# A two-layer transformer kernel: another order of the beginning, and the common row added beside the routed tiles

## The chip, the cores and the metric

The kernel runs on one core of a Trainium2 chip. The time is device microseconds (us) of one execution of the whole program, the median of several runs. TensorE (PE in the profile) does the matrix products; DVE, ACT and POOL are the vector, scalar and GpSimd engines; SP only issues transfers. ACT and POOL issue transfers of their own as well, each on a queue of its own.

## The reference

The activations x are 2 x 2048 rows (tokens) of 256 numbers. Two layers are applied, and each adds an attention part and a feed-forward part, both computed from the same normed input:

```python
xn = layernorm(x)
x = x + L0_attention(xn) + L0_ffn(xn)       # causal, one head, biases bq, bk, bv
xn = layernorm(x)
x = x + L1_attention(xn) + L1_ffn(xn)       # causal, then a block on selected tokens

def L0_ffn(xn):                             # mixture of experts
    scores = softmax(xn @ gate_w + gate_b)  # 8 experts, the best 2 of each token
    routed = sum(weight * expert(xn))       # silu(xn@w1+b1) * (xn@w2+b2) @ w3 + b3
    shared = mean over 2 shared experts     # same form, sw1, sb1, ... sb3
    return shared + routed
```

All of it is in float32. Layer 1's attention is causal over stretches of 512 tokens, and its feed-forward part works on the selected tokens alone. Neither is touched by the change.

## The kernel before

The tokens are held on the chip in eight blocks of 512 (`x_blocks`, four rows of 128 per block); blocks 0 to 3 are the first sequence, 4 to 7 the second. A tile is 128 tokens.

**The start (0 to 33 us).** `load_x` (L75) loads all eight blocks by SP. Two square weights, wq and wk, come by ACT's queue (L178), are transposed on TensorE (L409) and copied by ACT (L410). Scores need only their product wa (L491), so that keys are the normed input itself. The biases bq and bk lead to the small products of L433 and L438 and from these to a column `ca`, a scalar `qk_bias` and one more column of the value weights (L442 to L444, DVE). The value weights `wvg` hold wv, the gate's weights and this column. `every` is a row that is added to all tokens: the mean of the two shared experts' output biases, and bv (L421 to L424, POOL).

`moments` computes mean and variance of blocks (L205, L206, DVE), then the inverse root by a chain of small DVE operations (`rsqrt`, L189 to L194) and a shift (L214). `layernorm` makes the normed rows xn with ACT (L227), and turns them on TensorE (L233) into xnT. `prepare0(g)` calls it for block g, copies the normed rows as 16-bit halves for the scatter (L506, POOL), adds `every` to the block (L508, POOL, one operation of 128x1024), and makes values, gate scores and the score shift in four products, one for each j (L515), followed by `shift` (L523) and `logits` (L524) for the whole block. `evacuate` copies a result out of PSUM with DVE (L154) and ACT (L156) in turn. `project_q0` makes the queries of a block (L650, L654).

**Layer 0's attention (33 to 349 us).** It goes tile by tile: 0 to 15 of the first sequence, then 15 to 0 of the second. Scores come from L257, the row maximum from L268 and L274 (DVE), exp from L276 (ACT). The exponentials of the first four tiles are turned on TensorE (L321); for all others POOL splits them into two planes (L310), SP's queue transposes these by DMA (L312) into `across`, and DVE and ACT join them to pT (L287, L288). L332 multiplies with the values, L344 adds to x.

What else must be done in this time is a generator, `side0`: moments and `prepare0` of the other blocks (1 to 3 in one group, 4 to 7 in the next), the routing (`route_experts`), 64 scatters of rows on POOL (L636), and the fetch of the first two expert tiles. `beside()` takes steps of it at set rates (`BESIDE_L0`: 2.0, 1.2 and 0.72 steps per piece of attention); a step that yields `HOLD` keeps the instructions of the next step behind attention's latest ones. `before_tile` takes further steps until the values for a tile are there, and lets ACT's queue issue transfers from `clear()` that fill scratch memory with zeros (L454 and after; 13 of 768 KB, then others, then bias rows of the experts): two for each tile up to (0,7), then one.

**Routed experts (349 to 700 us).** 36 planned tiles of up to 256 rows. POOL joins the fetched rows to xT (L714), TensorE makes the two products of L722, ACT and DVE their activation and product (L836, L837), and TensorE the output (L844, DVE L849). The first tile's L722 products are interleaved with the end of attention (`fill_with_first`).

**After it** come the shared experts (to 1120 us) with layer 1's routing beside them, and layer 1 (to the end).

Between engines the order follows from data; within one engine it follows from the order in which the code is written and from manual dependencies.

## Time and profile before

| | us |
|---|---|
| median of 3 runs | 1507.68 (1506.83 to 1508.04) |
| the profiled execution's own time | 1504.37 |
| its span in the profile | 1502.7 |
| TensorE busy | 1453.6 |
| DVE busy | 696.2 |
| ACT busy | 437.5 |
| POOL busy | 401.2 |
| first values (L515) | 23.45 |
| first scores (L257) | 33.28 |
| first routed tile wholly after attention (L722) | 351.23 |

The profile holds one execution. Start times in it count from the start of its span. A matrix product in float32 leaves two records, a transpose one. TensorE's clock can be throttled; the granted clock is shown as a share of full speed (1.00), and its mean over the execution was 0.997. The time that an engine stands idle before an instruction is put down to whatever released it last.

### The profile page before, as it was taken

The numbers are of one execution on the slowest core, as the hardware profiler recorded it, in microseconds if no ns is written. First come the engines' busy times: TensorE is split into PE (matmuls) and PEld (weight loads), VectorE is DVE, ScalarE is ACT, GpSimd is POOL, SyncE is SP. The second block draws the span as 40 slices with busy tenths as digits, with TensorE's granted clock in tenths as the row PEclk, the third lists the DMA queues.
The fourth block names the chain that finished last, engine by engine and source line by source line (L and its number), as shares of the span: only waits on it lengthen the run. The fifth ranks groups of instructions, "written<-read, shape, count | busy, mean of one in ns | idle before, by whom it ended". The sixth has DMA issues, their size and how long they took to land.

```text
span 1502.7 us, 17818 instructions
## 1 busy us (share of the span) xinstructions
PE 1453.6 (97%) x5816; PEld 1033.6 (69%) x5816; DVE 696.2 (46%) x2064; ACT 437.5 (29%) x827; POOL 401.2 (27%) x581
## 2 busy tenths in 40 slices
PE   7989999999999999999999999999999998999999
PEld 4666666668888888887565656566675765667656
DVE  6437333443222222222424447766546458666354
ACT  2443333332111111111121121115524533344233
POOL 3454777531111111111201221132013122421122
PEclk9999999999999999999999999999999999999999
DMA  4744665586887989873101111130005435621153
GB/s 148 234 130 100 171 151 135 122 189 153 237 215 227 271 233 294 232 208 106 31 19 42 29 42 35 62 101 29 0 14 113 107 66 109 163 56 23 29 122 88
DMA packets 283201, 181.70 MB, mean 121 GB/s; under 512 B 185600, under 2 KB 258048, under 8 KB 283104
## 3 DMA queue, kind: packets, MB, share of 16 engines
q1 hardware_dynamic: 247280, 132.59, 35.9%
q10 hardware_dynamic: 28192, 27.06, 5.7%
q0 software_dynamic: 7632, 20.86, 4.5%
q8 instruction: 49, 0.80, 0.2%
q14 instruction: 48, 0.39, 0.1%
HBM read 93.14 MB, written 45.14 MB: 92 GB/s over the span
## 4 chain that ended last, share of the span: by engine, by line
PE 32%; DVE 8%; issue 6%; DMA 3%; ACT 2%; POOL 2%; POOLq 0%; SPq 0%; ACTq 0%; DVEq 0%
PE ps_tr L1469 6%; PE ps_sc L1469 6%; PE ps_pv L1488 5%; DMA across<-planes 3%; PE ps_pv L332 2%; PE ps_sc L257 2%; PE ps_mm L1340 2%; POOL planes L310 2%; PE ps_mm L1302 2%; DVE x L1499 1%; PE ps_tr L257 1%; PE ps_mm L1518 1%; PE ps_mm L932 1%; PE ps_mm L1323 1%; DVE row L268 1%
## 5 line engine op out<-in xcount | busy, mean ns | idle before, releaser
L310 POOL COPY planes<-row 128x512 uint16<-128x512 uint16 (+3 forms) x304 | 161.1, 577 | 271.7 <-ACT row L276 254.7
L288 ACT COPY pT<-across 128x512 uint16<-128x512 uint16 (+3 forms) x152 | 101.8, 684 | 210.8 <-DMA across<-planes 196.4
L257 PE MATMUL ps_sc<-xnT,qT 128*128 128x512 f32 (+3 forms) x384 | 161.7, 541 | 0.6 <-DVE qT L154 0.6
L837 DVE SCALAR_TENSOR_TENSOR hid<-ps_tr,be,act 128x256 f32<-128x256 f32 (+1 forms) x144 | 60.8, 464 | 180.1 <-PE ps_tr L722 178.8
L1458 POOL DMA_INDIRECT ya<-sorted_y,place x64 | 62.2, 972 | 307.0 <-DVE x L1499 225.6
L836 ACT ACTIVATE act<-ps_sc,be 128x256 f32<-128x256 f32 (+1 forms) x144 | 58.7, 459 | 280.8 <-PE ps_sc L722 280.8
L332 PE MATMUL ps_pv<-v,pT 128*128 128x256 f32 x544 | 127.6, 380 | 3.1 <-ACT pT L288 2.2
L722 PE MATMUL ps_sc<-xT,rw 128*128 128x256 f32 (+1 forms) x576 | 129.6, 368 | 0.6 <-issue 0.6
L722 PE MATMUL ps_tr<-xT,rw 128*128 128x256 f32 (+1 forms) x576 | 129.4, 367 | 0.0
L332 PE MATMUL ps_pv<-vg,pT 128*128 128x256 f32 x544 | 125.2, 380 | 2.9 <-ACT pT L288 2.8
L714 POOL COPY xT<-xs 128x512 uint16<-128x512 uint16 (+1 forms) x72 | 49.2, 728 | 291.1 <-DMA xs<-sorted_x 243.4
L844 PE MATMUL ps_pv<-rw,hid 128*128 128x256 f32 x544 | 124.8, 382 | 0.0
L1469 PE MATMUL ps_sc<-xnT,sw 128*128 128x512 f32 x256 | 121.9, 594 | 1.7 <-PEq L872 1.7
L1469 PE MATMUL ps_tr<-xnT,sw 128*128 128x512 f32 x256 | 122.0, 593 | 0.0
L332 PEld LDWEIGHTS ps_pv<-vg,pT 128*128 128x128 f32 x544 | 101.5, 189 | 26.1 <-ACT pT L288 7.0
L1488 PE MATMUL ps_pv<-sw,hid 128*128 128x256 f32 x512 | 117.5, 380 | 0.4 <-DVE hid L1477 0.4
L332 PEld LDWEIGHTS ps_pv<-v,pT 128*128 128x128 f32 x544 | 101.2, 190 | 23.7 <-issue 5.9
L722 PEld LDWEIGHTS ps_sc<-xT,rw 128*128 128x128 f32 x576 | 105.3, 190 | 14.3 <-POOL xT L714 0.9
L722 PEld LDWEIGHTS ps_tr<-xT,rw 128*128 128x128 f32 x576 | 105.1, 190 | 13.2
L844 PEld LDWEIGHTS ps_pv<-rw,hid 128*128 128x128 f32 x544 | 99.2, 190 | 19.3 <-DVE hid L837 5.7
L1488 PEld LDWEIGHTS ps_pv<-sw,hid 128*128 128x128 f32 x512 | 96.6, 190 | 19.1 <-issue 6.2
L1476 ACT ACTIVATE act<-ps_sc,sb 128x512 f32<-128x512 f32 x64 | 43.9, 686 | 219.5 <-PE ps_sc L1469 207.5
(336 smaller groups left out, 1969.9 us busy)
## 6 DMA issues: line engine op xcount, KB each, us to landing
rw<-in_rw SPq DMA_DIRECT2D x108, 512.0 KB, 4.6
sorted_x<-zero ACTq DMA_DIRECT2D x13, 768.0 KB, 5.4
sorted_y<-y SPq DMA_DIRECT2D x32, 256.0 KB, 4.2
be<-biases SPq DMA_DIRECT2D x36, 132.0 KB, 4.4
table<-xn SPq DMA_DIRECT2D x8, 514.0 KB, 3.5
x<-in_x SPq DMA_DIRECT2D x8, 512.0 KB, 6.8
gains<-zero ACTq DMA_DIRECT2D x8, 512.0 KB, 3.2
gain<-gains SPq DMA_DIRECT2D x16, 256.0 KB, 2.7
```

Of the source, the lines that this page charges most:

```text
L257: product = nc.tensor.matmul(ps[:, :w], lhsT=qT[:, dc, (i % 4) * P : (i % 4 + 1) * P], rhs=xnT[g0 + k][:, dc, :w], start=(dc == 0), stop=( ...
L288: nc.scalar.copy(words[:, :, 0], flat[:, w : 2 * w]),
L310: nc.gpsimd.tensor_copy(planes[:, h * w : (h + 1) * w], halves[:, :, 1 - h])
L332: product = nc.tensor.matmul(pv[:, :D], lhsT=turned[k][:, j : j + P], rhs=values[g0 + k][:, j // P, :D], start=(c + j == 0), stop=(c + j = ...
L714: nc.gpsimd.tensor_copy(words[:, :, :, 1 - k], xs[:, 2 * k : 2 * k + 2, :])
L722: product = nc.tensor.matmul(ps[:, k * n : (k + 1) * n], lhsT=we_in[:, dc, (h + k) * P : (h + k + 1) * P], rhs=xT[:, dc, :], start=(dc == ...
L836: activated = nc.scalar.activation(act, p1[:, at], AF.Silu, bias=b1[:, hc])
L837: nc.vector.scalar_tensor_tensor(hid[:, h + k, :], p2[:, at], b2[:, hc], act, op0=ALU.add, op1=ALU.mult)
L844: product = nc.tensor.matmul(po[:, r, :], lhsT=hid[:, hc, r * P : (r + 1) * P], rhs=w3[:, hc, :], start=(hc == 0), stop=(hc == 3),)
L1458: nc.gpsimd.indirect_dma_start(out=ya, out_offset=None, in_=sorted_y, in_offset=bass.IndirectOffsetOnAxis(ap=place[rank][:, t : t + 1], ax ...
L1469: product = nc.tensor.matmul(ps, lhsT=ww[:, dc, hc * P : (hc + 1) * P], rhs=xnT[g][:, dc, :], start=(dc == 0), stop=(dc == 1),)
L1488: product = nc.tensor.matmul(po[:, :D], lhsT=hid[:, hc, j * P : (j + 1) * P], rhs=w["sw3", n][:, hc, :], start=(hc == 0), stop=(hc == 3),)
```

## The change

At the start: SP loads x's first block, then wk, then the other blocks; wq stays first on ACT's queue, bk and bq move to POOL's, and bk is written as an additional column beside the turned wk. The product wa has that column too, and with it gives a column of wvg; the other bias products come behind it, and the scalar comes from a product on POOL (`both`) and one with ones. ACT's table is loaded by an exp of a single column (`warm`). The moments of block 0 alone come first, and its norm is divided between ACT and DVE. The four value products of block 0 are steps of `side0` now, and each counts in `made`, so that a tile waits only for its own. The score shift is a column of vg; the scalar is added together with the gate's bias (`besides`).

Beside attention: the groups of blocks are (1), (2), (3), (4, 5), (6, 7), and the moments of each are computed a group ahead. The zero fills begin with tile (0,4), two for each tile up to (0,11). Six empty steps come ahead of the scatters.

`every` is made at the beginning of the routed stage, and is added to x tile by tile, one addition of 128x256 on POOL behind each of the last 32 planned tiles' joins.

```diff
-    for g in range(NB):
-        load_x(g, nc.sync)
+    load_x(0, nc.sync)
...
+    first = []
-    def moments(blocks):
+    def moments(blocks, held_back=False):
...
-                nc.vector.bn_stats(stats[:, j, :], x_blocks[g][:, j, :])
+                i = nc.vector.bn_stats(stats[:, j, :], x_blocks[g][:, j, :])
+                if first:
+                    tc.add_manual_dep(i.ins, first[0].name, order, reason="the first block's norm goes first")
                 nc.vector.bn_aggr(mv[:, 4 * k + j, :], stats[:, j, :])
+                if held_back and j == 1 and g >= BPB:
+                    yield HOLD
             if g != blocks[-1]:
-                yield
+                yield HOLD if held_back else None
...
+        alone = not first
         for j in range(4):
-            nc.scalar.activation(
-                xn[:, j, :D], xb[:, j, :], AF.Identity, bias=shift[:, j : j + 1], scale=rstd[:, j : j + 1]
-            )
+            if alone and j % 2:
+                nc.vector.tensor_scalar(
+                    xn[:, j, :D], xb[:, j, :], rstd[:, j : j + 1], shift[:, j : j + 1], op0=ALU.mult, op1=ALU.add
+                )
+            else:
+                i = nc.scalar.activation(
+                    xn[:, j, :D], xb[:, j, :], AF.Identity, bias=shift[:, j : j + 1], scale=rstd[:, j : j + 1]
+                )
+                if alone:
+                    tc.add_manual_dep(i.ins, turned_last[0].name, order, reason="the weights are there first")
...
+        nc.gpsimd.dma_start(wk[:, :, D], a["bk0"])
+        bq = column("bq0", 2, "bq0", nc.gpsimd)
+        loaded = [weight(work, n, "qT", queue) for n, queue in (("wq0", nc.scalar), ("wk0", nc.sync))]
+        wvg = weight(wpool, "wv0", "wvg", cols=D + E + 1)
+        for g in range(1, NB):
+            load_x(g, nc.sync)
+        warm = const.tile([P, 1], F32, tag="warm", name="warm")
+        nc.vector.memset(warm, 0.0)
+        nc.scalar.activation(warm, warm, AF.Exp)
+        for _ in moments([0]):
+            pass
...
-        every = wpool.tile([P, 1, D], F32, tag="every", name="every")
-        parts = work.tile([P, 4, D], F32, tag="xn", name="parts", bufs=1)
...
+        besides = wpool.tile([P, E + 1], F32, tag="besides", name="besides")
+        nc.gpsimd.dma_start(besides[:, :E], a["gate_b"].partition_broadcast(P))
...
                 nc.tensor.matmul(
-                    ps[:, :D], lhsT=wq[:, ec, dc * P : (dc + 1) * P], rhs=wk[:, ec, :],
+                    ps[:, : D + 1], lhsT=wq[:, ec, dc * P : (dc + 1) * P], rhs=wk[:, ec, :],
                     start=(ec == 0), stop=(ec == 1),
                 )
             evacuate(wa[:, dc, :], ps[:, :D])
+            nc.vector.tensor_scalar(wvg[:, dc, D + E :], ps[:, D : D + 1], 1.0 / 16.0, None, op0=ALU.mult)
+        both = small.tile([P, 2], F32, tag="both", name="both")
+        nc.gpsimd.tensor_tensor(both, bq, wk[:, :, D], ALU.mult)
+        nc.gpsimd.tensor_tensor(both[:, 0:1], both[:, 0:1], both[:, 1:2], ALU.add)
...
+        nc.tensor.matmul(ps[:, 2:3], lhsT=ones, rhs=both[:, 0:1], start=True, stop=True)
+        nc.vector.tensor_scalar(ca, ps[:, 0:2], 1.0 / 16.0, None, op0=ALU.mult)
+        nc.vector.tensor_scalar(besides[:, E:], ps[:, 2:3], 1.0 / 16.0, None, op0=ALU.mult)
...
                 evacuate(vg[:, j, :], ps[:, : D + E + 1])
+                if g == 0:
+                    nc.vector.tensor_tensor(vg[:, j, D:], vg[:, j, D:], besides, ALU.add)
+                    made[0] += 1
                 yield
+                if j == 1:
+                    rows[g] = rows_pool.tile([P, 4, 2 * D], U16, tag=f"rows{g}", name=f"rows{g}")
...
             yield
+            yield from quiet(6)
...
         def side0():
-            for blocks in (range(1, BPB), range(BPB, NB)):
-                yield from moments(blocks)
+            yield from prepare0(0)
+            groups = [(1,), (2,), (3,), (4, 5), (6, 7)]
+            yield from moments(groups[0], True)
+            for k, blocks in enumerate(groups):
+                if k + 1 < len(groups):
+                    yield HOLD
+                    yield from moments(groups[k + 1], True)
                 for g in blocks:
                     yield from prepare0(g)
...
-            while values[b * BPB + i // 4] is None:
+            while made[0] <= (NB * 4 - 1 if b else i):
                 step()
...
-            if (b, i) > (0, 0):
-                clear_some(2 if i < 8 and b == 0 else 1)
+            if (b, i) >= (0, 4):
+                clear_some(2 if (b, i) < (0, 12) else 1)
...
+        every = hp.tile([P, D], F32, tag="every", name="every", bufs=1)
+        parts = hp.tile([P, 2, D], F32, tag="parts", name="parts", bufs=1)
+        for dst, src in ((parts[:, 0, :], a["sb3"][0]), (parts[:, 1, :], a["sb3"][1]), (every, a["bv0"])):
+            nc.gpsimd.dma_start(dst, src.partition_broadcast(P))
...
+            behind_start = at - (len(planned) - NB * 4)
+            if behind_start >= 0:
+                xt = x_blocks[behind_start // 4][:, behind_start % 4, :]
+                i = nc.gpsimd.tensor_tensor(xt, xt, every, ALU.add)
+                tc.add_manual_dep(i.ins, last_joined[0].ins.name, order, reason="one behind each tile's rows")
```

## The prediction

> **What bounds the kernel now.** I read the busy table and the slices first, then the waits and the order of time of the first 130 us, then the windows around the one long stall, then the passage from attention to the routed experts.

> ```profile
> span 1502.7 us, 17818 instructions
> PE 1453.6 (97%) x5816; PEld 1033.6 (69%) x5816; DVE 696.2 (46%) x2064; ACT 437.5 (29%) x827; POOL 401.2 (27%) x581
> ...
> PE   7989999999999999999999999999999998999999
> ```

> TensorE is the bound: 1453.6 of 1502.7 us. Little of its work goes (ten small records), so only its idle time and its time at half clock can be won. Idle time shows in the first three slices (7, 9, 8 tenths) and near the end, which the change leaves alone.

> ```profile
> 8.79 1.28 ACT L410 ACT_TABLE_LOAD   x1 [8.79 <-DMA qT<-in_wk]
> ...
> 10.56 0.59 ACT L410 COPY wk<-ps_mm 128x512 f32<-128x512 f32 x1
> 11.21 1.02 PE L433 MATMUL ps_mm<-bq,wk 128*128 128x1 f32 x4 [1.66 <-ACT wk L410]
> ...
> 15.50 2.05 PE L491 MATMUL ps_mm<-wk,wq 128*128 128x256 f32 x4
> ...
> 18.59 2.04 PE L491 MATMUL ps_mm<-wk,wq 128*128 128x256 f32 x4 [1.04 <-DVE rs_i L189]
> ...
> 22.60 0.69 DVE L154 COPY xnT<-ps_mm 128x512 f32<-128x512 f32 x1 [0.95 <-PE ps_mm L233]
> ...
> 23.45 3.90 PE L515 MATMUL ps_mm<-wvg,xnT 128*128 128x265 f32 x8 [0.68 <-ACT xnT L156]
> 24.08 2.35 POOL L508 TENSOR_TENSOR x<-x,every 128x1024 f32<-128x1024 f32 x1
> 24.22 2.23 DVE L193 SCALAR_TENSOR_TENSOR rs_t<-rs_t,ln_var 128x12 f32<-128x12 f32 x1
> ...
> 33.28 0.82 PE L257 MATMUL ps_sc<-xnT,qT 128*128 128x128 f32 x4
> ```

> This is the start in order of time (start, length, engine, line; in brackets the idle time before it and its releaser). ACT loads its table only when the first copy is due. Bias products stand ahead of wa (L491), and wa's second half waits until DVE, busy with the other blocks' moments, has read the bias bank at 18.4. Values start at 23.45 and scores at 33.28. A small DVE instruction (L193) takes 2.23 us because the common row's addition runs on POOL beside it; its twins take 0.13 to 0.15.

> ```profile
> DVE pT L287 <- DMA across<-planes: 8.3, 2, 4.7
> ...
> PE ps_mm L515 <- DVE xnT L154: 3.1, 1, 3.1
> ```
> ```profile
> 79.79 0.45 DVE L287 COPY pT<-across 128x512 uint16<-128x512 uint16 x1 [4.70 <-DMA across<-planes]
> ```
> ```profile
> 78.00:81.80 3.80, 0.69 (x3) 0.30 (x2) 2.00 (x7) 1.41 (x3) 1.31 (x2) 1.00 0.51 102
> 81.80:85.30 3.50, 3.40 (x9) 2.52 (x9) 1.06 (x3) 1.06 (x3) 1.86 (x4) 0.51 1.07 272
> ```

> The first fence gives total, count and longest wait. DVE waits in its queue for a transposed plane, with block 4's xnT copy behind it, and TensorE stands until 81.23. The window that follows runs at granted clock 0.51 (second column from the right but one), so about half of its 3.4 us is lost too: 3.1 + 1.7, and 0.2 around them, make this stall cost 5.0 us.

> ```profile
> 349.05 2.78 POOL L714 COPY xT<-xs 128x512 uint16<-128x512 uint16 x4 [6.70 <-PE ps_pv L332]
> ...
> 351.23 0.67 PE L722 MATMUL ps_sc<-xT,rw 128*128 128x256 f32 x2 [0.58 <-issue]
> ```

> The second routed tile's rows are joined on POOL only after attention's last products; TensorE idles 0.58.

> **The change part by part.**

> *Start, up to the first values: -4.5 us.* wk moves to SP behind x's first block. wq, first on ACT's queue, landed at 5.6, x's first block (512 KB) at 5.9 and its second at 8.45; half of that second load's time puts wk at 7.2, and wv beside it at 7.5. Its transposes take 1.1 (L409): 8.6. bk now comes by POOL's queue as 256 elements of four bytes, issued first. The nearest row is gate_b, issued first before, landed at 8.92; the last of the common row's loads there landed at 12.19. I take 8.9, being nearest in place, and keep 12.2 as end. The table load (1.28) and the first exp move ahead of 8, when ACT is idle. wk's copy (0.59) ends about 9.6, so wa starts at 9.8 against 15.50. It takes 2.05 + 2.04 and one column more, without the wait at 18.59, and ends at 13.9 at most. Eight bias records of the 20 (4.29 us) remain with two for the scalar: 10 × 0.215 = 2.1, to about 15.6. ca, qk's scalar and wvg's second column (three DVE operations of 0.13) follow; the second of wvg's columns gives back the bank for the transposes, so they start at 16.1 where 20.43 stood. DVE by then: eight statistics operations to 7.7, chain of 12 × 0.21 to 10.3, xn 1 and 3 (0.4 each, as L154's 128x256), eight constants moved ahead (0.1 each), to 11.9. So the norm isn't late. The transposes were paced by ACT's xn before (20.43 to 22.8); with all four there they need 8 × 0.23 = 1.9: 18.0, copies 0.69 and a little waiting: 19.0. Gain at L515: 23.45 - 19.0 = 4.45. Ends: 1.3 if bk lands at 12.2 (its 3.3 taken off 4.6), 6.0 if wk lands with wq.

> *Values per tile: 0.2.* Only j = 0 of the first block stands before qT; the six other pairs of records (12, 2.7 us at 0.224) move behind the first scores and aren't saved, since TensorE is the bound. The evacuation that waited for L193 goes: the wait was 0.38 net of queued work, I take 0.2. With cold records first, scores should begin near 26.5, 6.8 earlier, of which 2.7 is only moved. The clock's row: spacing of the L515 records falls from 0.44 to 0.22 us at 27.25, 3.8 after the first of them. If that lag keeps, the gain stands whole; if the clock opens where it did, on the same 3.41 us raster, cold work costs up to 1.5 more or 1.9 less, which is in the range.

> [...]

> *The stall at 78: -3.0 us.* POOL loses eight additions of 2.36 us (18.9 us between 24 and 112), which stood ahead of planes there. Blocks 4 to 7 are no longer normed in one group after block 3: DVE gets a group's moments ahead. In the new order some 14.4 us of products lie between the exp that feeds the late plane and the need of block 4's xnT, against 9.5: 4.9 more cover the 3.1 wait. I book 3.0 of 5.0: cover gone again, it is 0; whole, 5.0. What is late next is the plane of the tile behind it.

> *Moments later: 0.* 28 statistics of 0.41 and 0.16 and five chains of 12 × 0.17 make 26 us of DVE between 34 and 120, where it is busy 35.2 of 86 (the four windows there). 71% leaves room; the yields, ten instead of five, spread them. What hides it is that the blocks are due group by group; gone, one chain (2 us) shows per group, 10 us in all. POOL's remaining operations (rows, 2.0 each) may still stretch a chain's link to 2.2. I take 0, ends -1 and +4.

> *Zero fills from tile 4 on: 0.* They were 13 issues of 768 KB at 36 to 81, each filling all queues for about 2.3 us, landing in 5.4. They leave the tiles that turn straight on TensorE and meet, two by two, the plane transposes of tiles 4 to 11. A pair is 4.6 us of DMA work against 3.3 for an undisturbed transpose and 5.7 at the 78 stall, itself beside a fill. What covers it is the planes' lead, 5.7 to 9.4 us from exp to landing, under some 12 of products. Ends: -1, and +5 for each stall like that at 78. The bias rows, last in that chain of issues, go two tiles later and are due far after 300.

> *Common row in the routed stage: +0.7.* Three POOL issues (1.10 for two, 0.54) now stand ahead of the xT copies at 349, released by the same products: 1.64 less the 0.9 that POOL can do before TensorE needs that tile, 0.7, ends 0 and 1.6. The three sums (0.72, 0.87, 0.72) come behind the next copies. Then 32 additions of 0.72 (the 128x256 row of L422), 23 us beside POOL's 47.9 of 351 us: one per tile of 9.7 us, hidden. L837, DVE's product there, took 476 ns at the median and 486 at most with POOL's xT copies beside it, so POOL doesn't hold it up. Were each on the path: 23.

> [...]

> *The rest: 0.* The shift is a column now, logits are a copy of 0.18: one DVE operation for another. Six quiet steps delay the scatters by some 3 products; the rows of the first expert tile were ready about 20 us before they were needed. POOL's queue at the start (bk, bq, gate_b, router_b) carries four small issues for five. After 351 all orders are as they were but for the additions.

> Sum: -4.5 - 0.2 - 3.0 + 0.7 = -7.0. The profiled execution took 1504.4 (1.7 around the span) and is 3.3 under the median; it would come to 1497.4, the median to 1507.7 - 7.0 = 1500.7. A measurement of this kernel can tell about 0.2% (3.0 us) from no change.

> **Rivals.** *Given back (about same).* bk lands at 12.2, the gate of wk's copy, and the stall at 78 only moves: -1.3 - 0.2 + 0.7 = -0.8, 1506.9. For it: common-row loads on that queue took to 10.2 to 12.2. Against: bk is first in it, as gate_b was.

> *Fills beside transposes (slower).* The place is tiles 4 to 11: pairs of fills hold the queues 4.6 us, a plane lands 9 to 14 us after its exp, and TensorE stands as at 78, 5.0 each. The old stall stays (no -3.0), so -4.0 + 5n: one new stall is +1.0, two are +6.0, three +11.0, 1518.7. It decides from two on. For it: the only stall of this kind lay beside a fill, DMA share 1.07. Against: fills stood beside tiles 4 to 7 before too, and only one tile stalled.

> *More than forecast (faster).* wk lands early (6.0 in place of 4.5), the whole stall goes (5.0) and with it a quarter (2.0) of the other 8 us that TensorE idles between 33 and 120: -6.0 - 0.2 - 5.0 - 2.0 + 0.7 = -12.5: 1495.2.

> *It doesn't do what it says:* the scheduler keeps the moments of later blocks ahead of the first; the written dependencies exclude that.

> **How the numbers follow.** Forecast 0.54 (own range 1497 to 1504.5), given back 0.19, fills 0.15, more 0.12. Faster takes the 0.12 and 0.51 of the forecast: 0.63. Same takes 0.03 of it, 0.16 of given back and 0.02 of the fills with one stall: 0.21. Slower is 0.13 of the fills and 0.03 of given back with a late chain: 0.16. The range runs from 1494.5 (the better case) to 1511 (given back and a 4 us chain); only the fills' cases of two stalls and more lie above.

> **What would show it.** Right: wa's products near 10, values near 19, scores near 26 to 27, xnT of block 4 no longer waited for 3 us, L837 unchanged, TensorE idle about 1.3 at 349. Wrong: wk's copy waiting for bk beyond 11, a granted clock of 0.5 between 45 and 110, waits of pT for across in tiles 4 to 11, DVE operations of over 0.9 us among the moments.

## The result and the profile after

The changed kernel takes 1505.72 us (median of 20 executions, 1494.88 to 1511.60), the kernel before 1506.58 (20 executions, 1501.81 to 1511.13). The ratio is 0.9995, with a 95% interval of 0.9982 to 1.0008: no difference that can be told. The range of the prediction held the time, but its likeliest case, 7 us faster, did not come; what came is "about same", which had 0.21.

The profiled execution took 1503.70 us, with a span of 1501.5. From its page, the span, the busy time and the slices of TensorE:

```profile
span 1501.5 us, 17883 instructions
PE 1450.5 (97%) x5806; PEld 1033.4 (69%) x5806; DVE 702.8 (47%) x2110; ACT 437.2 (29%) x826; POOL 404.3 (27%) x609
...
PE   7899999999999999999999999999999998999999
```

Where the third slice (75 to 113 us) had 8 tenths, the second has it now. The start, in order of time:

```profile
8.40 0.59 ACT L436 COPY wk<-ps_mm 128x512 f32<-128x512 f32 x1 [1.48 <-DMA wk<-in_bk]
...
9.04 3.79 PE L489 MATMUL ps_mm<-wk,wq 128*128 128x257 f32 x8 [1.43 <-ACT wk L436]
...
15.16 1.94 PE L246 MATMUL ps_mm<-ident,xn 128*128 128x128 f32 x8 [0.41 <-DVE wvg L494]
...
17.03 1.84 PE L523 MATMUL ps_mm<-wvg,xnT 128*128 128x265 f32 x4
...
22.14 0.38 PE L272 MATMUL ps_sc<-xnT,qT 128*128 128x128 f32 x2
```

wa starts at 9.04 (before 15.50), values at 17.03 (23.45) and scores at 22.14 (33.28). The start therefore does more than was forecast: scores come 11.1 us earlier, and with 2.7 us of value products moved behind them 8.4 are left. (This is one execution; in the traces of the nine kernels with the new start, the experiments' included, scores begin between 20.7 and 23.8.) How this lead goes on can be read from the start of the update of x by DVE (L344 before, L359 after), tile by tile:

| update of x | before | after | difference |
|---|---|---|---|
| 4th tile | 72.9 | 59.7 | -13.2 |
| 11th | 153.4 | 143.2 | -10.2 |
| 24th | 313.6 | 303.3 | -10.3 |
| 26th | 329.5 | 323.2 | -6.4 |
| 32nd, the last of layer 0 | 349.0 | 342.4 | -6.5 |
| 33rd, the first of layer 1 | 1140.2 | 1134.7 | -5.5 |
| 54th | 1453.3 | 1450.5 | -2.8 |
| last | 1499.4 | 1498.1 | -1.3 |

(The tiles' products overlap, so that one row alone may be off by the order in which neighbours finish.) Some 10 us are won until the 24th tile. They are lost in three places: at the 25th and 26th tile, at the passage to the routed stage, and in layer 1, whose code is the same. And before the 11th tile there are stalls that the kernel before did not have. These are TensorE's waits between 34 and 135 us (line <- what it waited for: us in total, count, longest):

```profile
PE ps_mm L523 <- DVE xnT L153: 4.7, 2, 2.6
PE ps_mm L523 <- DVE pT L302: 2.1, 1, 2.1
PE ps_mm L585 <- DVE by L581: 1.1, 1, 1.1
PE ps_mm L523 <- DVE vg L153: 1.1, 1, 1.1
```

The stall at 78, its half clock included, is gone. In its place, values of later blocks wait three times for DVE (2.1 us at 57, 2.6 at 69 and 2.1 at 106). The second of these, in order of time:

```profile
66.05 2.43 POOL L536 COPY rows<-xn 128x1024 uint16<-128x1024 uint16 x2 [5.99 <-DVE nmx L289]
66.35 1.03 DVE L214 TENSOR_SCALAR ln_var<-ln_mv 128x8 f32<-128x8 f32 x1
...
67.49 1.01 DVE L187 TENSOR_TENSOR rs_i<-ln_var,halve 128x8 int32<-128x8 int32 x1
...
69.10 0.51 DVE L190 TENSOR_TENSOR rs_t<-rs_y 128x8 f32<-128x8 f32 x1
...
70.70 0.67 DVE L153 COPY xnT<-ps_mm 128x512 f32<-128x512 f32 x1
...
71.43 0.94 PE L523 MATMUL ps_mm<-wvg,xnT 128*128 128x265 f32 x3 [2.63 <-DVE xnT L153]
```

The chain of the next group's moments stands in DVE's queue ahead of this block's xnT, which had been ready since 68. Six of its links, 0.13 to 0.17 elsewhere, take 0.25 to 1.0 while POOL copies rows and planes, and each of the six ends within 0.03 us of the end of a POOL copy. At 57 such a chain stands there too, broken by a join of pT that waits 1.7 for its transposed plane. At 106 there is no chain; two joins of pT stand ahead of xnT, the first late by its plane, both stretched (0.45 is usual) beside POOL's row copies:

```profile
105.00 0.95 DVE L302 COPY pT<-across 128x512 uint16<-128x512 uint16 x1 [0.99 <-DMA across<-planes]
...
105.92 1.25 DVE L302 COPY pT<-across 128x512 uint16<-128x512 uint16 x1
...
107.06 0.67 DVE L153 COPY xnT<-ps_mm 128x512 f32<-128x512 f32 x1
```

The loss at the 25th tile:

```profile
309.39 0.52 ACTq L473 DMA_DIRECT2D biases<-in_rb  x1
310.00 0.76 ACT L303 COPY pT<-across 128x512 uint16<-128x512 uint16 x1 [2.40 <-DMA be<-biases]
...
310.82 2.68 PE L347 MATMUL ps_pv<-vg,pT 128*128 128x256 f32 x8 [1.95 <-ACT pT L303]
```

ACT should join a plane, whose DVE half was joined at 307. In its queue the issue of a bias row stands in front, and the profile puts ACT's idle time down to the landing of an earlier transfer of the experts' fetch (`be`), which reads the table `biases` that this issue writes. The windows around it, and two from layer 1 (length; busy time of PE, PEld, DVE, ACT, POOL; then the granted clock, the DMA share and GB/s):

```profile
308.56:311.98 3.42, 1.47 (x7) 1.05 (x6) 0.32 (x2) 1.65 (x3) 1.44 (x4) 1.00 0.97 190
311.98:315.39 3.41, 3.41 (x7) 2.03 (x6) 0.51 (x2) 0.00 (x0) 1.59 (x4) 0.50 1.12 101
1387.17:1390.58 3.41, 1.69 (x8) 1.14 (x9) 1.02 (x3) 1.68 (x5) 0.00 (x0) 1.00 0.01 2
1390.58:1394.00 3.42, 3.42 (x11) 2.60 (x10) 0.75 (x2) 0.00 (x0) 0.00 (x0) 0.50 0.00 0
```

In both pairs a window with little TensorE work is followed by one at half clock, in which half of 3.4 us, 1.7, is lost. The profile of after has four of these behind the start, that of before two. Three against one lie in layer 1, which makes 3.4 of the 4.2 us that are lost there. In the kernel before, no window of half clock followed the same wait in layer 1 (1.8 us at 1390): the window from 1389.16 held 1.57 us of TensorE, and the next was granted 1.00. So the granted clock has to be read beside each time. Over its 20 executions the changed kernel had a mean clock of 0.9938. The kernel before, in three sets of 20, 22 and 23 executions, had 0.9958, 0.9957 and 0.9958.

The passage to the routed stage:

```profile
342.95 1.16 POOL L845 DMA_DIRECT2D parts<-in_sb  x2 [7.12 <-PE ps_pv L347]
...
344.61 2.79 POOL L729 COPY xT<-xs 128x512 uint16<-128x512 uint16 x4
...
346.12 0.70 PE L739 MATMUL ps_sc<-xT,rw 128*128 128x256 f32 x2 [0.61 <-POOL xT L729]
```

The common row's loads stand ahead of the joins by 1.66 us. TensorE idles 0.7 and 0.6 where it idled 0.6 once.

### The profile page after: what moved, and what is told of

The parts are those of the page before. It is cut to its first block, busy times and chain, and to the rows that moved or that the text cites. A ratio compares the mean times of both kernels' runs of the same rounds, so it can differ in the third digit from the quotient of the medians.

```text
span 1501.5 us, 17883 instructions
## 1 busy us (share of the span) xinstructions
PE 1450.5 (97%) x5806; PEld 1033.4 (69%) x5806; DVE 702.8 (47%) x2110; ACT 437.2 (29%) x826; POOL 404.3 (27%) x609
## 4 chain that ended last, share of the span: by engine, by line
PE 35%; issue 7%; DVE 5%; POOL 2%; DMA 2%; ACT 1%; SPq 0%; POOLq 0%; ACTq 0%; DVEq 0%
PE ps_tr L1505 7%; PE ps_sc L1505 7%; PE ps_pv L1524 6%; PE ps_pv L347 3%; POOL planes L325 2%; PE ps_sc L272 2%; PE ps_mm L1376 2%; PE ps_mm L1338 1%; DMA across<-planes 1%; PE ps_mm L1554 1%; PE ps_tr L272 1%; PE ps_mm L968 1%; PE ps_mm L1359 1%; PE ps_mm L1430 1%; PE ps_mm L1442 1%
## 5 line engine op out<-in xcount | busy, mean ns | idle before, releaser
L868 DVE SCALAR_TENSOR_TENSOR hid<-ps_tr,be,act 128x256 f32<-128x256 f32 (+1 forms) x144 | 60.8, 464 | 180.2 <-PE ps_tr L739 178.8
L739 PEld LDWEIGHTS ps_sc<-xT,rw 128*128 128x128 f32 x576 | 105.3, 190 | 14.4 <-POOL xT L729 1.0
L739 PEld LDWEIGHTS ps_tr<-xT,rw 128*128 128x128 f32 x576 | 105.1, 190 | 13.2
L272 PEld LDWEIGHTS ps_sc<-xnT,qT 128*128 128x128 f32 x384 | 71.0, 192 | 54.1 <-issue 43.6
```

Of the source, the lines that this page charges most:

```text
L272: product = nc.tensor.matmul(ps[:, :w], lhsT=qT[:, dc, (i % 4) * P : (i % 4 + 1) * P], rhs=xnT[g0 + k][:, dc, :w], start=(dc == 0), stop=( ...
L739: product = nc.tensor.matmul(ps[:, k * n : (k + 1) * n], lhsT=we_in[:, dc, (h + k) * P : (h + k + 1) * P], rhs=xT[:, dc, :], start=(dc == ...
L868: nc.vector.scalar_tensor_tensor(hid[:, h + k, :], p2[:, at], b2[:, hc], act, op0=ALU.add, op1=ALU.mult)
```

## The experiments

The theory: the start's gain is real, and the changed kernel gives it back in named places: held moments, the bias row on ACT's queue, the loads at the passage, and more half clock behind each stall. The rivals: chance of the clock alone; or a limit by transfers that gives the start's gain back whatever is done. Each experiment has 6 to 12 executions, whose times lie 5 to 13 us apart; by this spread a difference between two medians below is uncertain by some 3 to 4 us either way.

**control**: the kernel before against itself.

> The kernel before against itself, for the granted clocks of its executions. The theory (the start's gain is real, and the changed kernel gives it back in new stalls, which also bring more windows of half clock): ratio 1.000 within 0.002, a mean granted clock near 0.996, above the 0.9936 of the changed kernel's 20 runs. The rival (the clock's windows fall by chance alone and strike both alike): a mean granted clock near 0.9936 here too.

Measured: 1506.11 us, ratio 1.0002 (0.9987 to 1.0017), mean clock 0.9955. The clock is that of the other sets of before, and above the changed kernel's 0.9938: the difference belongs to the kernel, not to chance alone.

**start_only**: the changed kernel with moments, fills and common row as before (and without the six empty steps ahead of the scatters).

```diff
...
+                    nc.gpsimd.tensor_tensor(
+                        x_blocks[g], x_blocks[g], every[:, 0:1, :].to_broadcast([P, 4, D]), ALU.add
+                    )
...
-            groups = [(1,), (2,), (3,), (4, 5), (6, 7)]
-            yield from moments(groups[0], True)
...
+            for blocks in (range(1, BPB), range(BPB, NB)):
+                yield from moments(blocks)
...
-            if (b, i) >= (0, 4):
-                clear_some(2 if (b, i) < (0, 12) else 1)
+            if (b, i) > (0, 0):
+                clear_some(2 if i < 8 and b == 0 else 1)
...
-                i = nc.gpsimd.tensor_tensor(xt, xt, every, ALU.add)
...
```

> The new start alone: loads, weights, block 0's norm and values as in the changed kernel; moments in two groups, zero fills and the common row as before (the row's loads in another buffer). The theory: first scores near 22 and, since DVE does the later moments early as before, most of the start's 8 us kept: 5 to 8 us faster than before, 1499 to 1502. The rival (what follows the start is set by transfers and takes the gain back whatever the moments do): 1505 to 1507, stalls before the values of later blocks as in the changed kernel. A second rival: the row's addition on POOL stretches block 0's neighbours as at 24 us before; then 2 to 3 us of the gain are missing at the third tile.

Measured: 1520.32 us, ratio 1.0093 (1.0075 to 1.0110), mean clock 0.988. The theory's number was missed by 19 us, and neither rival's came: the new start alone makes the kernel slower. The trace shows where (waits of TensorE from 24 to 130 us, then two lines in order of time):

```profile
PE ps_mm L530 <- DVE xnT L153: 9.4, 2, 5.6
PE ps_mm L530 <- DVE vg L153: 3.3, 2, 2.8
PE ps_mm L246 <- ACT xn L238: 2.9, 1, 2.9
```
```profile
31.26 2.08 ACT L238 ACTIVATE xn<-x,ln_shift,ln_rstd 128x256 f32<-128x256 f32 x4 [2.54 <-DVE ln_shift L218]
...
39.02 2.13 PE L530 MATMUL ps_mm<-wvg,xnT 128*128 128x265 f32 x4 [3.79 <-DVE xnT L153]
```

TensorE has no other work from 29.0 on, but block 1's norm is made from the chain for blocks 1 to 3, which ends at 31.1; then the chain of blocks 4 to 7 stands ahead of the xnT copy until 38.3. Four windows of half clock follow, from 31.2 to 44.8. So the changes do not add up one by one: by this trace the start needs another order of the moments behind it, which two_groups tests.

**row_moved**: the kernel before with the common row's move alone.

```diff
...
-            nc.gpsimd.tensor_tensor(
-                x_blocks[g], x_blocks[g], every[:, 0:1, :].to_broadcast([P, 4, D]), ALU.add
-            )
...
+                i = nc.gpsimd.tensor_tensor(xt, xt, every, ALU.add)
+                tc.add_manual_dep(i.ins, last_joined[0].ins.name, order, reason="one behind each tile's rows")
```

> The kernel before with the common row alone moved: made at the start of the routed stage and added beside 32 routed tiles. The theory: hidden but for about 1.1 us at the passage to the routed stage, and POOL, freed of 19 us beside attention, shortens the stall at 78 us by 0 to 5: between 4 us faster and 1 us slower, 1502.5 to 1507.5. The rival (the additions hold up DVE's product or the joins): 2 to 23 us slower, visible as a routed stage longer than 351 us.

Measured: 1501.43 us, ratio 0.9968 (0.9956 to 0.9980), mean clock 0.996. Faster by 4.8, a little more than the theory's end. The stall at 78 shrinks from 3.1 to 2.1, and the half clock behind it is gone in this profile, which has others in its place (one window at 48 us, three in layer 1):

```profile
80.00 0.71 PE L505 MATMUL ps_mm<-wvg,xnT 128*128 128x265 f32 x2 [2.08 <-DVE xnT L154]
```

Over its 9 executions the clock is that of the kernel before, so the 4.8 are not the clock's; the shorter stall shows 1.0 of them, and TensorE's idle time from 33 to 140 us falls from 8.6 to 5.8. The routed stage, from the first products to the shared experts', takes 364.1 us against 363.0. The additions are hidden but for the passage.

**moments_free**: the moments not held.

```diff
-            yield from moments(groups[0], True)
+            yield from moments(groups[0])
-                    yield HOLD
-                    yield from moments(groups[k + 1], True)
+                    yield
+                    yield from moments(groups[k + 1])
```

> The changed kernel with the moments not held behind attention's instructions (the five groups stay): DVE may do them as soon as it is free. The theory: the three stalls of 2.1 to 2.8 us before later blocks' values (7.1 us in all) shrink to 2 or less: about 5 us faster than the changed kernel, near 1500 to 1501, and fewer windows of half clock. The rival (moments are hidden as the prediction priced them, and those stalls come from late transposes by DMA in front of them in DVE's queue): no change, 1505 to 1506, the stalls where they were.

Measured: 1496.24 us, ratio 0.9937 (0.9917 to 0.9958), mean clock 0.9958: 9.5 us below the changed kernel, where 5 were expected. TensorE's waits from 34 to 135 us:

```profile
PE ps_mm L523 <- DVE xnT L153: 1.2, 2, 0.9
PE ps_mm L585 <- DVE by L581: 1.0, 1, 1.0
```

Of 9.0 us in four lines 2.2 are left, and the clock is that of the kernel before; the higher clock (0.0020 of 1500) is 3.0 of the gain. This is the largest of the costs. (The edit also takes away four of the steps inside the moments of blocks 4 to 7, so that all later side work comes some steps sooner; what that gives by itself was not tried.)

**rows_once**: what slows the held moments.

```diff
-                if j == 1:
+                if j == 1 and g:
+                    rows[g] = rows[0]
+                if j == 1 and not g:
```

> The changed kernel, in which POOL copies the normed rows of block 0 alone; the scatters of all blocks take those rows, so the experts' inputs are wrong and the 14 copies of 2.0 us of blocks 1 to 7 are left out. If the held moments cost what they cost because POOL's row copies stretch the chain and the pT copies on DVE (links of 0.4 to 1.0 us and pT of 0.95 and 1.25 in the changed kernel's trace), the stalls at 69 and 106 (2.8 and 2.3) shrink to under 1 each and the one at 57 (2.2) stays: 4 to 5 us faster than the changed kernel, near 1501. If the hold itself costs it (moments in DVE's queue ahead of the xnT copies), all three stay within 0.5 and the time is within 2 us of the changed kernel's 1505.7.

Measured: 1499.34 us, ratio 0.9948 (0.9929 to 0.9966), 6.4 below the changed kernel. TensorE's wait at 69 falls from 2.6 to 0.9 and that at 106 from 2.1 to 0.5 (at 101 now); the one at 57 stays (2.1 to 1.8); one of 2.5 comes at the routing near 121, where it was 1.1. In order of time, where the second stall was:

```profile
64.50 0.16 DVE L214 TENSOR_SCALAR ln_var<-ln_mv 128x8 f32<-128x8 f32 x1
...
64.77 0.16 DVE L187 TENSOR_TENSOR rs_i<-ln_var,halve 128x8 int32<-128x8 int32 x1
...
65.46 2.08 POOL L325 COPY planes<-row 128x512 uint16<-128x512 uint16 x4 [7.25 <-issue]
65.64 0.46 DVE L191 SCALAR_TENSOR_TENSOR rs_t<-rs_t,ln_var 128x8 f32<-128x8 f32 x1
```

Links that took 1.03 and 1.01 beside the row copies take 0.16; beside the plane copies they still take 0.4 to 0.5. The stall at 69 is thus the sum of both: a chain put ahead of xnT, and POOL's copies that stretch it. At 106 it is the joins of pT that the row copies stretch. Taking either the hold or the row copies away removes most of these two stalls; why the hold matters at 106, where no chain stands ahead, is not shown (without it the routing's work stands there already at 104). Nor does this run tell the stretching from a second effect: POOL, free of 14 us of copies (1.04 each; 2.0 is a pair), can also start its planes sooner.

In the changed kernel the six links that were stretched (0.25 to 1.03 us) each end with a POOL copy, within 0.03 us. In the routed stage no such stretch shows in DVE's product (L868, hid<-ps_tr,be,act): beside 32 additions of 724 ns it takes 476 ns at the median and 486 at most, exactly as before. What makes the two cases differ was not tried.

**row_back**: the changed kernel with the common row as before.

```diff
...
+                    nc.gpsimd.tensor_tensor(
+                        x_blocks[g], x_blocks[g], every[:, 0:1, :].to_broadcast([P, 4, D]), ALU.add
+                    )
...
-                i = nc.gpsimd.tensor_tensor(xt, xt, every, ALU.add)
...
```

> The changed kernel with the common row made and added as before, eight additions of 2.36 us on POOL beside the attention (its loads in another buffer), none beside the routed tiles. The theory (the row's move is worth what it gave the kernel before, 4.8 us, since POOL's additions delay planes and stretch DVE): 4 to 8 us slower than the changed kernel, 1510 to 1514. The rival (the gain of the move came from the one stall at 78, which the changed kernel has not): within 2 us of the changed kernel, or faster by the 1.1 at the passage to the routed stage.

Measured: 1511.94 us, ratio 1.0037 (1.0019 to 1.0054), 6.2 above the changed kernel, mean clock 0.992. The second stall grows from 2.6 to 4.7, and two new ones, 3.1 at 36 and 1.8 at 66, wait for the evacuation of a value:

```profile
77.05 2.34 POOL L544 TENSOR_TENSOR x<-x,every 128x1024 f32<-128x1024 f32 x1
77.14 2.27 DVE L190 TENSOR_TENSOR rs_t<-rs_y 128x8 f32<-128x8 f32 x1
...
80.12 1.25 PE L530 MATMUL ps_mm<-wvg,xnT 128*128 128x265 f32 x2 [4.74 <-DVE xnT L153]
```

The move of the row is worth about 5 to 6 us with the old start and with the new one.

**fills_sooner**: the bias rows' issues earlier.

```diff
-                clear_some(2 if (b, i) < (0, 12) else 1)
+                clear_some(2 if b == 0 else 1)
```

> The changed kernel with two zero fills for each tile up to (0,15), so that the bias rows, last in that chain on ACT's queue, are issued some four tiles sooner. In the changed kernel ACT's join of pT at 310.0 stands behind such an issue, which waits for an earlier transfer of its lane, and TensorE idles 2.1 there. The theory: that stall goes, and with it a window of half clock in some executions: 2 to 3.5 us faster than the changed kernel, 1502 to 1504. The rival (the stall is the late transpose itself, or other transfers take the place): no change.

Measured: 1502.67 us, ratio 0.9966 (0.9947 to 0.9984), 3.1 below the changed kernel, mean clock 0.9944. The wait of 2.0 at the 25th tile is gone: between 300 and 345 us TensorE's waits are

```profile
PE ps_pv L347 <- DVE x L359: 0.5, 1, 0.5
PE ps_sc L272 <- ACT qT L669: 0.4, 1, 0.4
```

and the three early stalls stand as they were (2.1, 2.6, 2.1). The gain is about as large as its uncertainty; what the trace shows is that the stall itself went. (In the changed kernel's trace the wait at 310 ended with a transfer of `be`, which reads `biases`; that the two share a lane isn't shown.)

**three_mended**: moments free, fills sooner, and the row's loads behind the second tile's join.

```diff
-            yield from moments(groups[0], True)
+            yield from moments(groups[0])
...
-                clear_some(2 if (b, i) < (0, 12) else 1)
+                clear_some(2 if b == 0 else 1)
...
+            if at == 1:
+                for dst, src in ((parts[:, 0, :], a["sb3"][0]), (parts[:, 1, :], a["sb3"][1]), (every, a["bv0"])):
+                    i = nc.gpsimd.dma_start(dst, src.partition_broadcast(P))
+                    tc.add_manual_dep(i.ins, last_joined[0].ins.name, order, reason="behind the second tile's rows")
...
```

> The changed kernel with three of its costs taken out: moments not held, fills two for each tile up to (0,15), and the common row's loads behind the second tile's join instead of ahead of it. Theory: what moments_free gave (1496.2) less 2 to 3.5 for the bias rows and 1.0 for the passage: 1491.5 to 1493.5. The rival (the time is set by the windows of half clock, whatever stalls are left): 1495 to 1497, as moments_free.

Measured: 1491.84 us (1488.13 to 1495.35), ratio 0.9894 (0.9874 to 0.9915), mean clock 0.9963: 14.6 us below the kernel before, 13.9 below the changed one, and in the theory's interval. The three costs add up (9.5, 3.1 and about 1), within the uncertainty.

**fills_early**: the changed kernel with the fills where they were before.

```diff
-            if (b, i) >= (0, 4):
-                clear_some(2 if (b, i) < (0, 12) else 1)
+            if (b, i) > (0, 0):
+                clear_some(2 if i < 8 and b == 0 else 1)
```

> The changed kernel with the zero fills where they were before: from tile (0,1), two for each tile up to (0,7), then one. By the prediction (the shift costs nothing by itself) and by fills_sooner (what the shift costs is the late end of the chain, the bias row at 309): 2 to 3.5 us faster than the changed kernel, 1502 to 1504, as fills_sooner, with the stalls at 57, 69 and 106 where they are. By the rival of fills beside transposes: 5 or more faster, and the stall at 57, whose pT waits for a transpose, goes. A third case: fills of the first tiles collide with the loads of x, and the values of block 1 or 2 come later: slower than the changed kernel.

Measured: 1510.32 us, ratio 1.0017 (1.0002 to 1.0032), 4.6 above the changed kernel, mean clock 0.9925. Only the third case has the sign. Its reason doesn't hold: x had landed by 20.8, and the first fill is issued at 25.8. The waits at 57 and 69 grow from 2.1 to 3.1 and from 2.6 to 2.8, the one at the routing from 1.1 to 2.9, and a wait of 1.5 for ACT's join of pT stays (at 316). The one at 106 is gone: there xnT is copied ahead of the joins. The first fills stand on ACT's queue between the exps and block 1's norm (issues of 0.7 to 1.4 us), and xn starts at 30.3 where it started at 27.3. That this is what shifts the later stalls was not tried and stays open. Collision of later fills with transposes, which the prediction priced as a rival, isn't what costs here: with the fills put back the kernel is slower and TensorE idles 11.8 us instead of 9.8 from 22 to 140. For the stall at 106 alone it stays possible; two fills were issued at 95, ahead of its late plane.

**two_groups**: moments in two groups, not held; else the changed kernel.

```diff
-            groups = [(1,), (2,), (3,), (4, 5), (6, 7)]
...
+            for blocks in (range(1, BPB), range(BPB, NB)):
+                yield from moments(blocks)
```

> The changed kernel with the later moments in two groups as before (1 to 3, 4 to 7), not held and not a group ahead; fills and the common row as in the changed kernel. Against moments_free (1496.2) only the grouping differs. The theory (with scores from 22 on, block 1's norm is due before 12 rows of statistics and their chain are done, so start_only's first stalls, 2.9 and 4.1 us near 31 to 39 and the half clock behind them, come from the grouping): 6 to 12 us slower than moments_free, 1502 to 1508. The rival (start_only's stalls come from the common row's additions and the early fills): within 2 us of moments_free.

Measured: 1507.52 us, ratio 0.9995 (0.9982 to 1.0008), 11.3 above moments_free, mean clock 0.9933. The grouping decides, as the theory has it, but the places are others than expected: a stall of 1.5 for xn near 30, one of 3.1 for a value's evacuation near 62, 2.8 at the routing, and 3.8 us by the clock (0.0025 of 1500).

The steps from moments_free to start_only can be summed: grouping 11.3, row 6.2, fills 4.6 make 22.1; measured are 24.1 (1520.3 - 1496.2). That the last two were measured with held moments, and that start_only also leaves out six empty steps, makes this a rough check only.

## Why the prediction was right or wrong

The range held the time, and the gain did not come. That it held is luck: the start and the stall at 78 gave 13.4 us where the sum had 7.7, and costs of about 13.5, of which the sum had 0.7, took it back. The likeliest case was wrong by its step on the moments, and two smaller ones.

- *Start, -4.5 and -0.2*: right in mechanism, too small. 8.4 were won in the profiled execution. Values came 6.4 earlier instead of 4.5. wa's products began at 9.04 (taken 9.8): bk gated wk's copy as forecast, but at 8.4 (taken 8.9), and wk was there before it (its transposes began at 6.49, taken was 7.5). Another 1.0 is the copy of xnT's first half (at 16.29), which runs beside the second half's transposes; the sum had it behind all eight. The rest came between values and scores, 1.2 of it by the clock, which was full 1.4 us behind the first values where 3.8 was taken. That is one throw: in the nine traces of this start the first full clock comes between 12.7 and 21.4 us, in four of them before the first values. Two slips: 13.9 and 2.1 make 16.0, not 15.6; and the end of -6.0 doesn't follow, since with bk at 8.9 an earlier wk gains nothing.
- *Stall at 78, -3.0*: the whole 5.0 went, half clock included. Part of it is the row's move (row_moved: 4.8 in all, 1.0 of it in this stall).
- *Moments later, 0 with +4 as the end*: this step failed. The DVE share was computed and looked low enough; what counts is the place in DVE's queue. A chain of 12 dependent links, held behind attention's instruction, stood in front of the xnT copy that TensorE needed (at 57 and 69), and POOL's row copies stretched it. The prediction named a link of 2.2 beside POOL's copies but didn't multiply it by the links or put it ahead of xnT. Cost: 9.5 (moments_free), 3.0 of it by the clock. Two of its own signs came: DVE operations of over 0.9 us among the moments (1.03, 1.01), and pT waiting for `across` (1.7 at 56, 1.0 at 105).
- *Zero fills, 0*: off on both sides. With held moments the shift is worth 4.6 (fills_early), more than the -1 allowed. Its tail costs about 3.1 (fills_sooner): "due far after 300" looked at when the rows are used; what mattered is that their issue stands in ACT's queue and waits there (2.40 us ahead of the join at 310.00).
- *Common row, +0.7 at the passage, additions hidden*: right. The waits there are 0.8 longer (0.7 + 0.6 - 0.6), and mending it is part of three_mended.
- *The clock*: the prediction priced half clock at the start and behind the stall at 78 alone. A new stall of about 2 us brought a window of half clock or did not: 1.95 us at 310.82 was followed by one, 2.63 at 71.43 was not. Over all executions it is 0.0020 of the clock, 3.0 us.

Of the rivals, "given back" names the outcome (1506.9), but not its mechanism: bk did gate wk's copy, but at 8.4 and not at 12.2, and the stall at 78 didn't move but was replaced. Fills beside transposes don't explain the whole (fills_early is slower); at most the stall at 106 is of that kind.

## What to carry to other kernels

That an engine is busy only 70% of the time does not say that moved work is hidden on it: look at what a moved chain will stand in front of in its queue, and count for each link what POOL does beside it (here 1.03 us beside a row copy, 0.16 without). A transfer's issue can hold what stands behind it in its queue, however late its data are due: here ACT stood idle 2.40 us ahead of the join at 310.00. Where small stalls decide, read the granted clock of several executions beside the time: the stall of 1.95 us at 310.82 was followed by a window at half clock, another 1.7, and one of 1.83 at 1304.90 was not.
